# Loads of grouped-query attention: from the wide to the narrow query blocks, with four query buffers

## The chip, the cores and the metric

The kernel runs on one core of a Trainium2 chip. The metric is the device time of one execution in microseconds; the median of the runs shown stands for a kernel. A core has TensorE (matrix products, "PE" in the profile), VectorE ("DVE"), ScalarE ("ACT"), GpSimd ("POOL") and SyncE ("SP"). In this kernel SP does nothing but issue DMAs, one after the other, in the order of the program; all transfers go through this one queue, and 16 DMA engines carry them out.

## What is computed

A gated block on 1024 rows of 512 values: layer norm, then attention with 32 query heads and 8 key/value heads (RMS-normed queries and keys, a linear bias by distance, causal) and a quantized feed-forward network side by side; the attention's output is multiplied by a silu of the network's, and the input is added.

```python
xn = _layernorm(x, axis=-1)
# attention
q = (xn @ Wq.T) ...   # 32 heads of 128
k, v = xn @ Wk.T, xn @ Wv.T ...   # 8 heads of 128: four query heads share one
q, k = _rmsnorm(q, q_norm_w), _rmsnorm(k, k_norm_w)
scores = jnp.einsum('bkgqd,bksd->bkgqs', qg, k) / math.sqrt(HD)
bias = jnp.where(rel > 0, NEG_INF, slopes[:, :, None, None] * rel)
attn = jax.nn.softmax(scores + bias[None], axis=-1)
s = jnp.einsum('bkgqs,bksd->bkgqd', attn, v) ... @ Wo.T
# feed-forward network on xn, weights dequantized by groups of 128
g = _silu((silu(xn @ gate_proj) * (xn @ up_proj)) @ down_proj)
return x + s * g
```

## The kernel before

**Stages.** The feed-forward network runs first (to about 280 us), and its gate silu(...) is stored to the DRAM scratch `gd`. Then come twelve projections (for each pair of key/value heads one "kv" and two "q"), whose results are normed, split into a high and a low 16-bit half, transposed by DMA (`transposed`, L752) and stored to `kd`, `vd` and `qd`. From 423 us on attention runs, at first beside the last two projections.

**Steps of attention.** There are eight groups of heads (g = 0 to 7), each with four blocks of 256 queries (`qb`) and four heads per block and two tiles of 128 queries per head: 256 steps, 32 a group, 8 a block. A step makes the scores of one head and one tile against all keys up to it, so its width is 128 to 1024 keys. Blocks 2 and 3 (widths 640 to 1024) are called wide, blocks 0 and 1 (128 to 512) narrow. Groups 1 to 6 go in the order 2, 3, 0, 1 (`ORDER`): in a group, steps 0 to 15 are wide and 16 to 31 narrow. Group 0 goes 3, 2, 1, 0 and group 7 goes 2, 3, 1, 0. "Step 20 of group 4" below is step 4 * 32 + 20 = 148 of the loop. In the first three groups the bias lets far keys be left out for some heads; groups 3 to 6 have the same full widths.

**One step** (`step(n)`). On TensorE the scores of step n (`scores`), then part of the product with the values for step n - 9 (`values`, `AV_LAG`), then parts of the output projection (`out_proj`). On VectorE `biased` (L1041), one step behind, and `split_lo` (L1074), four steps behind; on ScalarE `exponentials` (L1047) and `split_hi` (L1066). At the end of `split_lo` SP issues the DMA transpose of the split probabilities, L1082, or L1077 for block 0, where one transpose serves both tiles of a head. The product with the values waits for that transpose. So a transpose of step n stands on the queue with the instructions of step n + 4, and its result is wanted at n + 9. The split probabilities lie in five buffers (`P16_BUFS`), the transposed ones in four.

**Other DMAs, all on the same queue.** Per group 512 KB of keys (`load_keys`, L952) at step 4 of the group before, 512 KB of values (`load_values`, L956) at its step 24, and 512 KB of queries a block (`load_queries`, L964), at step 2 of the block before; there are two query buffers. Group 6's queries are stored untransposed, and its loads are two DMA transposes from DRAM a block (L962). Group 7's are never stored: `halves` of the last projection leaves them in SBUF (`last_pairs`), and `last_queries` (L974) transposes them tile by tile into the query buffers, at the steps in `LAST_QUERIES`. When VectorE makes these halves stands in `LAST_PAIRS` (the step is that number plus 8). The output projection's weights of a group are four tiles of 256 KB (`load_wo`, L991), loaded ten steps before the first product, that is at steps 8, 10, 12 and 14 of the group; GpSimd scales them at steps 10 to 16 (L994), ScalarE and GpSimd split them at steps 12 to 18 (L1000, L1001). For the end, `gate_load` (L1131, L1132) brings back 512 KB of the gate and 512 KB of x for each of the four blocks, at steps 211, 219, 235 and 251 (`GATE_LOADS`), into the buffers "f" that the projections used; `gate_partial` on GpSimd uses them at the steps in `GATE_SUMS`.

Of the kernel before, what the change touches and what calls it, by code (L numbers as in the profile page):

```python
# [11 lines left out]
F32 = mybir.dt.float32  # L12
# [10 lines left out]
P = 128  # L23
S = 1024
DM = 512
H = 32
HKV = 8
NH = 4
# [8 lines left out]
NQT = QB // P  # L37
# [10 lines left out]
ORDER = ((2,), (3,), (0,), (1,))  # L48
LAST_ORDER = ((2,), (3,), (1,), (0,))

AV_LAG = 9

KEYS_STEP = 4
VALUES_STEP = 24


LAST_ROOTS = {1: 24, 0: 36}
LAST_PAIRS = {4: 46, 5: 78, 6: 110, 7: 142, 2: 174, 3: 221, 0: 224, 1: 229}
LAST_QUERIES = {4: 217, 5: 219, 6: 225, 7: 227, 2: 233, 3: 235, 0: 241, 1: 243}

WO_SPLIT = 6
WO_SCALE = 8
WO_LOAD = 10

GATE_LOADS = [211, 219, 235, 251]
GATE_SUMS = [227, 235, 251, 259]
PF_BUFS = 5
P16_BUFS = 5
OH_BUFS = 8
# [40 lines left out]
def attention_gated_by_ffn_kernel(ctx, tc, x, gu_w, gu_z, gu_s, dn_w, dn_z, dn_s, wq, wkv, wo, qnw, knw, out):  # L110
    nc = tc.nc
    ve, se, ge, te, sp = nc.vector, nc.scalar, nc.gpsimd, nc.tensor, nc.sync
# [4 lines left out]
    rings = {}  # L117
# [62 lines left out]
    gd = dram.tile([NT, P, DM], F32, name="gd")  # L180
# [645 lines left out]
    for it in range(NI):  # L826
        for tb in range(2):
# [14 lines left out]
            for i in range(4):  # L842
                c = slice(i * P, i * P + P)
# [36 lines left out]
    for tag, cols, bufs in (  # L880
        ("f", 2048, 4),
        ("ss", HT * NH, 3),
        ("ms", HT * NH, 2),
        ("inv", HT * NH, 2),
        ("nwt", HT * NH, 2),
        ("a16", 512, 5),
        ("tr", 512, 5),
        ("k2", 256, 1),
    ):
        ring(tag, fq, cols, bufs)  # L890
# [14 lines left out]
    def pieces(tag, cols):  # L905
        return [slot[:, c : c + cols] for slot in rings[tag].slots for c in range(0, slot.shape[1], cols)]

    wh_pieces = pieces("wh", QB // 2)
    rings["oh"], rings["ol"] = Ring(wh_pieces[:OH_BUFS]), Ring(wh_pieces[OH_BUFS:])
    rings["wor"] = Ring(pieces("wl", DM))  # L910
    free_pieces = pieces("v16", DM // 2) + pieces("sq", DM // 2)
# [2 lines left out]

    def y_rows(t):
        return y_halves[t // HT][:, t % HT * DM : (t % HT + 1) * DM]

    def queue_half(p, half):

# [24 lines left out]
    NB = S // QB  # L944
    blocks = [(g, qbs) for g in range(HKV) for qbs in (FIRST_ORDER if g == 0 else ORDER if g < HKV - 1 else LAST_ORDER)]
    units = [(g, qb, hh) for g, qbs in blocks for hh in range(NH) for qb in qbs]
    kT, vT, qT, woh, wol = {}, {}, {}, {}, {}
    trel, pT, oT, wor = {}, {}, {}, {}

    def load_keys(g):  # L950
        kT[g] = rings["kT"].take(F16, NT, 2, P)
        sp.dma_start(kT[g].rearrange("p t a k -> p t (a k)"), kd[g // 2][:, g % 2])  # L952

    def load_values(g):
        vT[g] = rings["vT"].take(F16, NT, 2, HD)
        sp.dma_start(vT[g].rearrange("p t a d -> p t (a d)"), vd[g])  # L956
# [32 lines left out]
    def load_wo(g, i):  # L989
        wor[g, i] = rings["wor"].take(F32, DM)  # L990
        sp.dma_start(wor[g, i], wo[(g * NH + i) * HD : (g * NH + i + 1) * HD, :])  # L991
# [133 lines left out]

    gates = {}

    def gate_load(qb):
        gx = rings["f"].take(F32, 2, NQT, DM)
        t0 = qb * NQT  # L1130
        sp.dma_start(gx[:, 0], gd[t0 : t0 + NQT].rearrange("t p c -> p t c"))  # L1131
        sp.dma_start(gx[:, 1], x[t0 * P : (t0 + NQT) * P, :].rearrange("(t p) c -> p t c", p=P))  # L1132
        gates[qb] = gx

    def gate_partial(qb, i):

        gx, yt = gates[qb], y_rows(qb * NQT + i)
        ge.tensor_tensor(yt, yt, gx[:, 0, i], ALU.mult)
        ge.tensor_tensor(yt, yt, gx[:, 1, i], ALU.add)
# [17 lines left out]
    nn, BS = len(order), NH * NQT  # L1157
# [2 lines left out]
    begin, free = 0, 0  # L1160
    for k, (g, qbs) in enumerate(blocks[:-1]):
        steps = BS * len(qbs)
        for qb, lead in zip(blocks[k + 1][1], (6, 10) if steps > BS else (2, 5)):
            q_at.setdefault(begin + lead, []).append((blocks[k + 1][0], qb))
        begin += steps
        due = begin + AV_LAG + 1
        n, taken, done = max(free, due), 0, 0
        op_first.setdefault(g, n)
        for qb in qbs:
            for i in range(NQT):  # L1170
                for part in range(NH):
                    op_at.setdefault(n, []).append((g, qb, i, part))
                    if part == NH - 1:
                        acc_at.setdefault(n + 1, []).append((g, qb, i))
                    taken, done = taken + 1, done + 1

                    if taken == 2 or n < due + done:
                        n, taken = n + 1, 0
        free = n + (taken > 0)
    near = [False]  # L1180
    TILES = NT * len(projections)

# [20 lines left out]
    def step(n):  # L1203
        nonlocal last_ps
        if n < nn:
            u, qt = order[n]
            g, qb, hh = units[u]
            for due in q_at.get(n, ()):
                if due[0] < HKV - 1:
                    load_queries(*due)  # L1210
            for t, due in LAST_QUERIES.items():
                if due == n:
                    last_queries(t)
            if g + 1 < HKV:
                if n % (NB * BS) == KEYS_STEP:
                    relative(g + 1)
                    load_keys(g + 1)
                elif n % (NB * BS) == VALUES_STEP:
                    load_values(g + 1)
            scores(u, qt)  # L1220
        done = at(n - AV_LAG - 1)
        done = done[0] if done and done[1] == NQT - 1 else None
        if done is not None:
            heads_hi(done)
        for stage, lag in ((biased, 1), (exponentials, 1), (split_hi, NQT + 1), (split_lo, NQT + 2)):
            advance(stage, n - lag)
        if done is not None:
            heads_lo(done)
        if n < nn + AV_LAG + 1:
            for due in acc_at.get(n, ()):  # L1230
                accumulate(*due)
        finish_step()

        def project():
            for due in op_at.get(n, ()):
                out_proj(*due)

        if at(n - AV_LAG):
            values(*at(n - AV_LAG), project)
        else:  # L1240
            project()
        if done is not None and units[done][:2] == final:
            g, qb, hh = units[done]
            if hh == 0:
                last_ps = [ps2()[:, 0, :] for i in range(NQT)]
            for i in range(NQT):
                out_proj(g, qb, i, hh)
            if hh == NH - 1:
                for due in acc_at.get(nn + AV_LAG + 1, ()):
                    accumulate(*due, other=True)  # L1250
                for i in range(NQT):
                    accumulate(g, qb, i)
        if n in GATE_LOADS:
            gate_load(LAST_ORDER[GATE_LOADS.index(n)][0])
        for i in range(NQT):
            if n - i in GATE_SUMS:
                gate_partial(LAST_ORDER[GATE_SUMS.index(n - i)][0], i)
        for lead, act in ((WO_SPLIT, split_wo), (WO_SCALE, scale_wo), (WO_LOAD, load_wo)):
            for g, first in op_first.items():
                if n + lead - first in range(0, 2 * NH, 2):  # L1260
                    act(g, (n + lead - first) // 2)
# [3 lines left out]
    def project_all(k):  # L1265
        p = projections[k]
        for t in range(NT):
            prepare(k + 1, t)
            if k + 2 < len(projections):
                if t < KT:  # L1270
                    projections[k + 2].load(t)
                n = projections[k + 2].n
                for i in (range(n + 1)[: n // 2], range(n + 1)[n // 2 : n - n // 4], range(n + 1)[n - n // 4 :])[t - 5] if t >= 5 else ():
                    projections[k + 2].squares(i)
            if t == HT:
                p.undo()
                if k == len(projections) - 3:
                    load_keys(0)
                    for qb in blocks[0][1]:
                        load_queries(0, qb)  # L1280
                elif k == len(projections) - 2:
                    load_values(0)
            if (k, t) == (len(projections) - 3, HT + 1):
                wo_squares_sums()

            row = t if k < len(projections) - 1 else (t + HT) % NT
            p.tile(row)
            finish_step()
            if t % HT == HT - 1:
                queue_half(p, row // HT)  # L1290
            c = (k - len(projections) + 2) * NT + t
            if c >= 0:
                for due in q_at.get(c // 2, ()) if c % 2 == 0 else ():
                    load_queries(*due)
                if c == 2 * KEYS_STEP:
                    relative(1)
                    load_keys(1)
                early_tile(c)
# [74 lines left out]
```

## Time and profile before

The three runs took 1016.07, 1020.3 and 1016.7 us, median 1016.7. The profiled execution took 1020.44 us.

| What | us or share |
|---|---|
| Profiled execution / span from first to last instruction | 1020.44 / 1018.6 |
| Granted TensorE clock, mean | 0.989 |
| TensorE / VectorE / ScalarE / GpSimd busy | 95% / 84% / 76% / 42% |
| DMA transposes of probabilities: issued / median to landing | 224 / 3.9 to 4.0 |
| GpSimd's wait for weights of the output projection (L994) | 130.0 |
| Group 4: wide steps / narrow steps | 38.4 / 29.9 |
| Group 6: wide steps / narrow steps | 38.4 / 36.9 |
| From the start of group 7's last block (979.2) to the end | 39.4 |

The profile is a page for one execution: busy times, the span in 40 slices, the chain of work that ended last (followed back from the last instruction to what released each), groups of like instructions, and DMA issues. The trace behind it can be asked for windows, for a timeline and for waits. A window line has start and end, its length, then for each engine the busy time and in brackets the number of instructions, then the granted TensorE clock, the mean busy share of the DMA engines (over 1 where packets of one engine overlap) and GB/s. A timeline line has the start, the time taken (of several merged instructions, from the first's start to the last's end), engine, line and what is written from what. For SP "q" marks its sequencer: the time taken is that of issuing.

### The profile page before, as it was taken

The page shows a single profiled execution, that of the slowest core. Times are in us where ns is not written, and L with a number is a line of the kernel's source. Part 1 is how long each engine was busy: PE and PEld are TensorE (multiplying, and loading weights), DVE is VectorE, ACT ScalarE, POOL GpSimd, SP SyncE. Part 2 cuts the span into 40 slices and gives each one's busy share as a digit, 9 for nine tenths or more (in the row PEclk, how much of TensorE's full clock was granted, in tenths as well). Part 3 has the DMA queues.
Part 4 walks back from the last instruction along what each step waited for, and adds up shares of the span by engine and source line. Part 5 has one row for each costly group of instructions (what it writes and reads, how often), then busy time and mean ns, then how long its engine had stood idle before and what let it go on. Part 6 is the DMA issues. An engine that isn't in the chain of part 4 may idle for free. (4 is left out here: it accounts for less than half of the span.)

```text
span 1018.6 us, 17980 instructions
## 1 busy us (share of the span) xinstructions
PE 964.7 (95%) x5688; PEld 561.8 (55%) x5688; DVE 857.2 (84%) x1764; ACT 775.5 (76%) x2160; POOL 429.4 (42%) x424
## 2 busy tenths in 40 slices
PE   6899999999999999996998999999999999989995
PEld 4344477854444444444555666665676666656562
DVE  7888998728888878877898998987989989969985
ACT  5777745778878887787887987987879978858861
POOL 2588764216666555564235151051241421530722
PEclk9999999999999999999999999999999999999999
DMA  7132359535998999998898999997999999999994
GB/s 251 37 121 93 104 170 310 187 125 163 204 273 190 245 229 215 236 237 202 172 196 161 206 216 183 227 203 158 231 202 191 212 201 190 202 219 198 218 201 108
DMA packets 425063, 195.74 MB, mean 192 GB/s; under 512 B 371522, under 2 KB 382078, under 8 KB 424958
## 3 DMA queue, kind: packets, MB, share of 16 engines
q1 hardware_dynamic: 424958, 194.50, 85.5%
q8 instruction: 46, 0.75, 0.3%
q14 instruction: 59, 0.48, 0.1%
HBM read 76.27 MB, written 27.27 MB: 102 GB/s over the span
## 5 line engine op out<-in xcount | busy, mean ns | idle before, releaser
L1074 DVE SCALAR_TENSOR_TENSOR p<-pf,row,p 128x384 f16<-128x384 f32 (+7 forms) x256 | 208.8, 816 | 20.9 <-ACT p L1066 18.0
L1047 ACT ACTIVATE pf<-pf,row 128x384 f32<-128x384 f32 (+7 forms) x256 | 184.9, 723 | 41.6 <-DVE row L1041 37.3
L1041 DVE CUSTOM_DVE_ANT_0 pf<-s,trel,cs 128x384 f32<-128x384 f32 (+7 forms) x256 | 191.4, 748 | 19.8 <-PE s L153 19.7
L1066 ACT ACTIVATE p<-pf,row 128x384 f16<-128x384 f32 (+7 forms) x256 | 184.0, 719 | 6.3 <-DMA pT<-p 1.4
L151 PE MATMUL s<-kT,qT 128*128 128x512 f16 (+3 forms) x356 | 115.3, 324 | 11.8 <-DVE row L1041 11.5
L994 POOL TENSOR_SCALAR wl<-wl,rvs 128x512 f32<-128x512 f32 x32 | 53.7, 1677 | 149.0 <-DMA wl<-in_wo 130.0
L152 PE MATMUL s<-kT,qT 128*128 128x512 f16 (+3 forms) x356 | 115.4, 324 | 0.0
L153 PE MATMUL s<-kT,qT 128*128 128x512 f16 (+3 forms) x356 | 114.0, 325 | 0.0
L716 POOL TENSOR_TENSOR f<-f,inv 128x512 f32<-128x512 f32 (+1 forms) x96 | 102.1, 1084 | 1.4
L151 PE MATMUL m<-v,wh 128*128 128x512 f16 x248 | 95.0, 383 | 0.0
L153 PE MATMUL m<-v,wh 128*128 128x512 f16 x248 | 94.9, 383 | 0.0
L151 PE MATMUL o<-pT,vT 128*128 128x256 f16 (+1 forms) x302 | 79.6, 264 | 13.9 <-DMA pT<-p 13.7
L151 PEld LDWEIGHTS <-vT 128*128 128x128 f16 x594 | 58.9, 99 | 57.8 <-DMA pT<-p 15.1
L1110 ACT ACTIVATE wh<-o 128x256 f16<-128x256 f32 x128 | 47.7, 373 | 54.4 <-PE o L153 53.8
L152 PEld LDWEIGHTS <-vT 128*128 128x128 f16 x594 | 58.9, 99 | 41.4 <-issue 4.5
L152 PE MATMUL o<-pT,vT 128*128 128x256 f16 (+1 forms) x302 | 79.6, 264 | 0.0
L153 PE MATMUL o<-pT,vT 128*128 128x256 f16 (+1 forms) x302 | 79.3, 264 | 0.0
L151 PE MATMUL o<-wide,vT 128*128 128x256 f16 (+1 forms) x292 | 75.9, 260 | 3.1 <-DMA wide<-p 3.1
L152 PE MATMUL o<-wide,vT 128*128 128x256 f16 (+1 forms) x292 | 75.9, 260 | 0.0
L153 PE MATMUL o<-wide,vT 128*128 128x256 f16 (+1 forms) x292 | 75.7, 260 | 0.0
L151 PE MATMUL m<-wh,xth 128*128 128x512 f16 x192 | 72.8, 379 | 1.2 <-ACT h L869 1.2
L153 PE MATMUL m<-wh,xtl 128*128 128x512 f16 x192 | 72.8, 379 | 0.0
(200 smaller groups left out, 2531.4 us busy)
## 6 DMA issues: line engine op xcount, KB each, us to landing
qd<-tr SPq DMA_DIRECT2D x48, 256.0 KB, 3.3
qT<-qd SPq DMA_DIRECT2D x24, 512.0 KB, 4.4
wide<-in_wq SPq DMA_DIRECT2D x32, 256.0 KB, 3.7
wo_sq<-in_wo SPq DMA_DIRECT2D x8, 1024.0 KB, 7.8
wl<-in_wo SPq DMA_DIRECT2D x32, 256.0 KB, 3.6
gui<-in_gu_w SPq DMA_DIRECT2D x13, 512.0 KB, 3.7
wide<-in_wkv SPq DMA_DIRECT2D x16, 256.0 KB, 3.8
vd<-v SPq DMA_DIRECT2D x8, 512.0 KB, 4.7
```

Of the source, the lines that this page charges most:

```text
L151: te.matmul(ps, lhsT=lh, rhs=rh, start=first, stop=False)
L152: te.matmul(ps, lhsT=lh, rhs=rl, start=False, stop=False)
L153: te.matmul(ps, lhsT=ll, rhs=rh, start=False, stop=last)
L716: ge.tensor_tensor(f, f, ib, ALU.mult)
L994: ge.tensor_scalar(wor[g, i], wor[g, i], rvs[:, g : g + 1], None, ALU.mult)
L1041: ve.tensor_tensor_reduce(p, ps, trel[g][:, S - w :], cs[:, hh : hh + 1], 3e38, ALU.add, ALU.min, least[:, c])
L1047: se.activation(p, p, AF.Exp, bias=least[:, c], scale=-1.0, accum_out=total[:, c])
L1066: se.activation(p16[u, qt][:, :, 0, :], pf[u, qt], AF.Copy, scale=scale[:, qt : qt + 1])
L1074: ve.scalar_tensor_tensor(lo, p, scale, hi, ALU.mult, ALU.subtract)
L1110: se.activation(oh, av_ps[u], AF.Copy, scale=1.0 / P_SCALE)
```

## The change

Four things change.

1. For groups 3 to 7 the loads get new steps, counted in the group before: keys at 20 (was 4), values at 26 (was 24). For groups 3 to 6 the queries of blocks 2, 3, 0, 1 go to steps 21, 22, 28 and 33 (were 26, 34, 42 and 50). The output projection's weights of groups 3 to 6 go to steps 23, 25, 27 and 29 of the group before (were 8, 10, 12 and 14 of their own), those of group 7 to steps 0, 2, 4 and 6 of group 7. Groups 0 to 2 keep their steps.
2. The query ring gets two more buffers, which are the transpose buffers "tr" of the projections under another name.
3. The gate and x loads are cut in four of 256 KB per block: block 2's at steps 20, 22, 24 and 26 of group 3, block 3's at the same steps of group 4, block 1's at those of group 5, block 0's at steps 234 to 240. What uses them keeps its steps.
4. The last projection's late halves move from steps 229, 232 and 237 to 215, 220 and 222, and group 7's transposes of queries from 217 to 243 to 212 to 227.

```diff
-KEYS_STEP = 4
-VALUES_STEP = 24
+RELATIVE_STEP = 4
+LOADS_IN_NARROW = 3
+KEYS_STEP = 4, 20
+VALUES_STEP = 24, 26
+QUERIES_STEPS = (26, 34, 42, 50), (21, 22, 28, 33)
+WO_STEPS = 40, 23, 32
...
-LAST_PAIRS = {4: 46, 5: 78, 6: 110, 7: 142, 2: 174, 3: 221, 0: 224, 1: 229}
-LAST_QUERIES = {4: 217, 5: 219, 6: 225, 7: 227, 2: 233, 3: 235, 0: 241, 1: 243}
+LAST_PAIRS = {4: 46, 5: 78, 6: 110, 7: 142, 2: 174, 3: 207, 0: 212, 1: 214}
+LAST_QUERIES = {4: 212, 5: 213, 6: 216, 7: 217, 2: 220, 3: 221, 0: 226, 1: 227}
...
-WO_LOAD = 10
-
-GATE_LOADS = [211, 219, 235, 251]
-GATE_SUMS = [227, 235, 251, 259]
+GATE_LOADS = {2: [116, 118, 120, 122], 3: [148, 150, 152, 154], 1: [180, 182, 184, 186], 0: [234, 236, 238, 240]}
+GATE_SUMS = {2: 227, 3: 235, 1: 251, 0: 259}
...
-        ("tr", 512, 5),
+        ("tr2", 1024, 2),
+        ("tr1", 512, 1),
...
+    rings["qT"].slots += rings["tr2"].slots
...
+    rings["tr"] = Ring([*pieces("tr2", 512), *pieces("tr1", 512)])
...
-    def gate_load(qb):
-        gx = rings["f"].take(F32, 2, NQT, DM)
-        t0 = qb * NQT
-        sp.dma_start(gx[:, 0], gd[t0 : t0 + NQT].rearrange("t p c -> p t c"))
-        sp.dma_start(gx[:, 1], x[t0 * P : (t0 + NQT) * P, :].rearrange("(t p) c -> p t c", p=P))
-        gates[qb] = gx
+    def gate_load(qb, i):
+        if i == 0:
+            gates[qb] = rings["f"].take(F32, 2, NQT, DM)
+        gx, t = gates[qb], qb * NQT + i // 2
+        sp.dma_start(gx[:, i % 2, i // 2], x[t * P : (t + 1) * P, :] if i % 2 else gd[t])
...
-        for qb, lead in zip(blocks[k + 1][1], (6, 10) if steps > BS else (2, 5)):
-            q_at.setdefault(begin + lead, []).append((blocks[k + 1][0], qb))
+        if g == 0 and blocks[k + 1][0] == 0:
+            q_at.setdefault(begin + 2, []).append((0, blocks[k + 1][1][0]))
...
+    key_at, value_at, wo_at = {}, {}, {}
+    for g in range(HKV):
+        ahead = (g - 1) * NB * BS
+        steps = QUERIES_STEPS[g >= LOADS_IN_NARROW]
+        if g:
+            for step_, (qb,) in zip(steps, ORDER):
+                q_at.setdefault(ahead + step_, []).append((g, qb))
+            key_at[ahead + KEYS_STEP[g >= LOADS_IN_NARROW]] = g
+            value_at[ahead + VALUES_STEP[g >= LOADS_IN_NARROW]] = g
+        for i in range(NH):
+            wo_at[ahead + WO_STEPS[(g >= LOADS_IN_NARROW) + (g == HKV - 1)] + 2 * i] = g, i
```

More of the change, by code (lines that the diff above doesn't have):

```diff
@@ L1214, in step @@
             if g + 1 < HKV:
-                if n % (NB * BS) == KEYS_STEP:
+                if n % (NB * BS) == RELATIVE_STEP:
                     relative(g + 1)
-                    load_keys(g + 1)
-                elif n % (NB * BS) == VALUES_STEP:
-                    load_values(g + 1)
+            if n in key_at:
+                load_keys(key_at[n])
+            if n in value_at:
+                load_values(value_at[n])
             scores(u, qt)
@@ L1252, in step @@
                     accumulate(g, qb, i)
[L1253 to L1258, printed above, removed]
+        for qb, steps in GATE_LOADS.items():
+            if n in steps:
+                gate_load(qb, steps.index(n))
+        for qb, due in GATE_SUMS.items():
+            if 0 <= n - due < NQT:
+                gate_partial(qb, n - due)
+        if n in wo_at:
+            load_wo(*wo_at[n])
+        for lead, act in ((WO_SPLIT, split_wo), (WO_SCALE, scale_wo)):
             for g, first in op_first.items():
@@ L1294, in project_all @@
                     load_queries(*due)
-                if c == 2 * KEYS_STEP:
+                if c == 2 * RELATIVE_STEP:
                     relative(1)
```

## The prediction

> **What bounds the kernel now.** I read the page's busy line first, then windows cut at the wide and narrow steps, then the chain of waits, then SP's timeline.
>
> ```profile
> PE 964.7 (95%) x5688; PEld 561.8 (55%) x5688; DVE 857.2 (84%) x1764; ACT 775.5 (76%) x2160; POOL 429.4 (42%) x424
> GB/s 251 37 121 93 104 170 310 187 125 163 204 273 190 245 229 215 236 237 202 172 196 161 206 216 183 227 203 158 231 202 191 212 201 190 202 219 198 218 201 108
> qT<-qd SPq DMA_DIRECT2D x24, 512.0 KB, 4.4
> wl<-in_wo SPq DMA_DIRECT2D x32, 256.0 KB, 3.6
> ```
>
> TensorE is busy for 95%, so a change of loads can win only what TensorE waits. The windows say where that is; they alternate between a group's wide and narrow steps, from group 3 to group 7.
>
> ```profile
> 631.60:670.00 38.40, 38.40 (x261) 23.74 (x259) 37.47 (x72) 34.69 (x69) 10.33 (x6) 1.00 1.08 209
> 670.00:703.20 33.20, 31.17 (x224) 20.78 (x222) 25.11 (x70) 23.16 (x66) 8.28 (x9) 0.95 0.93 183
> ...
> 741.60:771.50 29.90, 29.60 (x225) 20.19 (x224) 25.31 (x70) 23.28 (x66) 8.32 (x9) 1.00 1.01 197
> ...
> 809.90:840.10 30.20, 29.49 (x225) 20.18 (x223) 25.12 (x68) 23.17 (x66) 8.26 (x9) 1.00 1.03 195
> 840.10:878.50 38.40, 38.40 (x260) 23.74 (x258) 37.49 (x72) 34.69 (x69) 11.15 (x6) 1.00 1.00 196
> 878.50:915.40 36.90, 31.39 (x224) 20.69 (x222) 24.98 (x67) 22.63 (x63) 14.15 (x14) 0.95 1.04 206
> 915.40:958.50 43.10, 40.54 (x261) 24.31 (x259) 42.70 (x78) 34.96 (x70) 15.71 (x9) 0.96 1.08 212
> 958.50:979.20 20.70, 19.58 (x144) 13.22 (x142) 18.14 (x38) 16.83 (x38) 6.41 (x5) 1.00 1.12 197
> ```
>
> Wide steps take 38.40 us in groups 3 and 6 alike, with TensorE never idle and VectorE busy for 37.5: nothing is to be had there. Narrow steps take 29.9 in group 4 with 0.30 idle, so about 29.6 is their floor; group 3 takes 33.2, group 6 takes 36.9. Group 7's wide steps take 4.7 more than 38.40, with VectorE at 42.70 of 43.10. The chain of waits names what TensorE lacked in the narrow steps:
>
> ```profile
> 681.05 5.80 DMA pT<-p
> ...
> 752.40 4.37 DMA pT<-p
> ...
> 884.84 6.06 DMA pT<-p
> ...
> 893.54 5.48 DMA pT<-p
> ```
>
> These are transposes of the last wide steps, wanted at narrow steps 21 to 23. SP's timeline shows why group 6 fares worst, and what stands before the last block's transposes:
>
> ```profile
> 883.19 5.42 SPq L1082 DMA_TRANSPOSE pT<-p  x2
> 888.65 2.98 SPq L962 DMA_TRANSPOSE qT<-qd  x2
> 891.73 4.61 SPq L1082 DMA_TRANSPOSE pT<-p  x2
> ...
> 988.61 0.53 SPq L1131 DMA_DIRECT2D f<-gd  x1
> 989.19 0.48 SPq L1132 DMA_DIRECT2D f<-in_x  x1
> 990.14 1.84 SPq L1077 DMA_TRANSPOSE wide<-p  x1
> ```
>
> VectorE had finished the halves for the transpose at 891.73 by 884.87: it was held 6.9 us behind 2.98 us of query transposes and a slow queue. In group 4 the matching one starts 1.4 us after its halves (749.39 after 748.00), and most others within 0.1 us: there VectorE paces the queue, and an earlier free queue gains about a microsecond, not five.
>
> **The change, part by part: what it removes.** All against the profiled execution's own 1018.6 us of span.
> (a) Narrow steps of groups 3, 4 and 5. Weights (4 x 256 KB) and two query loads (2 x 512 KB) leave the sixteen steps before the late transposes. Those then follow VectorE, and the excess over 29.6 goes: 3.6 + 0.3 + 0.6 = 4.5. Group 2's narrow steps (29.1) wait for VectorE, 0.8 us; nothing is taken.
> (b) Narrow steps of group 6. The query transposes at 888.65 move into group 5, the 1 MB of gate and x at 896.39 into group 3: 36.9 - 29.6 = 7.3.
> (c) Wide steps of group 7. Three halves leave, each a cast of 0.484 us and a subtraction of 0.804 (the rows of L729 and L730 at 512 elements): 3 x 1.29 = 3.9 of VectorE, which is busy there 42.70. That leaves 38.8, just above the 38.40 that TensorE needs; with the bubbles between them I take 39.1, a gain of 4.0 (ends: 0, should another VectorE wait take their place, to 4.7). 1 MB of gate loads and four query transposes leave too; the weights only move eight steps up.
> (d) Group 7's block 1 takes 20.7 with 1.1 idle on transposes; the two query transposes in front of them go: 1.1.
> (e) The end. The transpose at 990.14 stands behind 1 MB and lands after 6.7 us; the two issued at 981.41 and 982.76 land after 3.7 and 3.5. TensorE's idle time for it is 2.3, its landing 3 us late: I take 2.5 (ends 0 and 3.5).
> Sum (a) to (e): 19.4.
> The earlier weights also end GpSimd's wait (130 us in nine waits at L994) and ScalarE's for it (5.7 us at L1000). Both are idle time off the path, taken as nothing; if ScalarE's were on it, it would be 5.7 more. Two more query buffers cost nothing to fill; their memory was the projections' transposes', long read before step 10 first takes it.
>
> **What it adds.** The loads land in the narrow steps behind the last wide transpose: step 19 issues that, and keys stand at step 20. Behind each load are block 0's and block 1's transposes, and for these wait TensorE and, through five probability buffers, ScalarE and then VectorE.
> Bytes first. Group 4's narrow steps move 197 GB/s x 29.9 us = 5.9 MB. Keys, one query load more, four weights and four gate pieces add 0.5 + 0.5 + 1 + 1 = 3 MB or, in bytes, 3.1 MB. That makes 9.0 MB in 29.6 us, 304 GB/s; the page's best slice has 310. So it just fits, with no reserve. Group 2 gets no gates: 2.1 MB more, some 270 GB/s. A single load: 256 KB lands in 3.6 us and 512 KB in 4.4, so 512 KB hold the queue some 1.6 us (estimate: twice the difference).
> The slack: group 4's last transpose of block 0 is issued at 764.95, lands at 768.00 and is used at 771.14, 3.1 us later; the next is issued at 768.14, lands at 771.34 and is used at 774.07, 2.7 later. About 1 MB stands newly before each pair of steps there (weights, a query load, a gate piece), 3.2 us against a slack of 2.7 to 3.1. SP itself has room: 0.55 to 0.67 us an issue, beside transposes of 1.23 each in steps of some 1.5.
> (f) Group 2: 0.3 (ends 0 and 2). (g) Groups 3 and 4: 1.2 each (ends 0, the late loads hidden by the slack, and 5, all of the 9.6 us of added transfer less two slacks). (h) Group 5 loads group 6's queries by DMA transposes, six before its end at 1.3 us of SP each instead of three loads at 0.57: 6.1 us more on SP, of which the gaps between issues take about half: 3 (ends 0 and 7.3, which is what group 6 pays for such a pair today). (i) Group 6: keys, six query transposes of 1.26 us and VectorE's 3.9 us in a stretch where it is busy 25.0 of 29.6, so it reaches 28.9, nearly full: 2 (ends 0 and 7).
> Sum: 0.3 + 2.4 + 3 + 2 = 7.7; the ends are 0 and 26.
> For scale, a rule: the Trainium skill (DMA: Bandwidth & Descriptors, Latency and other measured facts) gives DMA transposes 261 GB/s where the middle dimension is not contiguous, and its section Anatomy of one DMA a variable part of bytes / 436 GB/s. Taking 4.3 MB of group 4's narrow bytes as transposes and the other 4.7 as loads, that makes an estimate of 16.5 + 10.8 = 27.3 us, which would fit with 2 us to spare and put (g) at 0; the row's 310 GB/s has no transposes to speak of in it, and the slower of the two is kept.
> The clock prices a wait a second time. Group 3's narrow steps lose 3.6 us for 2.0 idle, at a granted clock of 0.95; group 4's and 5's, with waits of 0.3 and 0.7, lose no more than these at 1.00. The new waits are nearer to those, so 7.7 stands; at group 3's ratio of 1.8 it would be 13.9. The skill (TensorE: Matmul & The Clock Gate, Part 1: The HAM clock gate) says that the clock halves after an idle window of about 3.4 us. By that rule, too, waits this short are not paid twice.
>
> **The numbers.** 1018.6 - 19.4 + 7.7 = 1006.9 of span. The profiled execution took 1.8 more than its span (1020.44): 1008.7. It lies 3.7 above the median of 1016.7; group 3's stall, which its like in groups 4 and 5 do not have, is about that size, and it is among what goes. So I carry the time over without a shift: **1008.5 us**, 8.2 below the median.
>
> **Rivals.**
> *The room in the narrow steps is used up* (20%). Every load falls due before the queue has caught up, and (f) to (i) come near 16: 1020.4 - 19.4 + 16 = 1017, no change. For it: 304 of 310 GB/s, and a DMA share already at 1.01 to 1.04 in these steps. Against it: the share passes 1.08 in wide steps without TensorE waiting.
> *The loads were hidden anyway* (12%). In groups 3 to 5 VectorE, not the queue, makes the transposes late, (a) is zero, (c) half: 1020.4 - 12.9 + 4 = 1011.5. For it: most transposes start within 0.1 us of their halves. Against: 5.8 us of transfer in group 3 where 3 to 4 is usual.
> *Slower: SP's order in the narrow steps* (13%). One mechanism: transposes of blocks 0 and 1 are pushed past their 2.7 to 3.1 us, the five probability buffers stay full, ScalarE and VectorE stop, and the score matmuls after them, as group 6 shows today at 7.3 us. If groups 3 to 6 each pay that: 1020.4 - 19.4 + 4 x 7.3 + 0.3 = 1030.5. It decides once loads and query transposes ahead of one transpose pass 3 us.
> *The forecast* (55%): its own range is 1002 to 1013, from (f) to (i) near 1 and near 12.
>
> The overall range is 1000 to 1020: below, all gains at no cost (1020.4 - 19.4 = 1001), above, the first rival with some to spare; part of the slower case, a tenth, and a little below are left out. About 0.5% (5 us, 1011.6 and 1021.8) is what a measurement can tell from no change here. Faster by more: most of the forecast's 55%, half of the second rival and a little of the first, 0.60. Same: 0.26. Slower: 0.14, the last rival and the tail of the first.
>
> **What would show it.** Windows: narrow steps of groups 3 and 6 at 30 to 32 us, group 7's wide steps near 39, the stretch from the last block on at some 37. The chain should no longer name transposes at the ends of wide blocks; if it names those of blocks 0 and 1, or ScalarE waiting for pT at L1066, the costs were too low. SP's timeline should show late transposes following the halves within 0.1 to 1.5 us. I am wrong if narrow steps of groups 3 to 5 pass 33 us, or if group 7's wide steps stay at 43.

## The result, and the profile after

The changed kernel takes 1021.21 us, the one before 1017.33 (medians of 20 runs each on the same chips); the ratio is 1.0041, 95% interval 1.0028 to 1.0054. It is slower by 0.4%, where 0.8% faster was forecast. The profiled execution after took 1021.26 us, span 1019.5. From the page, the busy line and the shares of the chain that ended last, by engine:

```profile
PE 962.9 (94%) x5688; PEld 560.1 (55%) x5688; DVE 859.9 (84%) x1764; ACT 775.9 (76%) x2160; POOL 426.0 (42%) x424
...
PE 32%; DMA 6%; DVE 3%; ACT 3%; issue 2%; SPq 2%; POOL 1%; DVEq 0%; ACTq 0%
```

TensorE's share fell by one point. In the chain DMA has 6% (4% before), and SP's queue, which did not appear, has 2%: the wait for transposes did not go, it grew. The windows of the profile after, cut as before (narrow steps of group 2, then wide and narrow steps of groups 3 to 6, then group 7's wide steps, its block 1, and the last block to the end):

```profile
603.26:633.10 29.84, 28.61 (x215) 18.88 (x213) 25.34 (x71) 23.35 (x67) 8.14 (x9) 1.00 1.09 235
633.10:672.26 39.16, 38.58 (x261) 23.66 (x259) 37.28 (x70) 34.72 (x67) 10.29 (x6) 1.00 0.99 190
672.26:701.73 29.47, 29.47 (x224) 20.14 (x222) 25.14 (x70) 23.20 (x66) 8.22 (x9) 1.00 1.07 270
701.73:742.04 40.31, 38.58 (x260) 23.66 (x258) 38.02 (x72) 34.75 (x69) 10.29 (x6) 1.00 0.96 176
742.04:772.28 30.24, 29.79 (x225) 20.18 (x223) 25.80 (x71) 23.58 (x67) 8.22 (x9) 1.00 1.09 251
772.28:812.78 40.50, 38.75 (x260) 23.57 (x258) 37.32 (x70) 34.72 (x67) 10.83 (x6) 1.00 1.04 183
812.78:847.80 35.02, 31.13 (x225) 20.69 (x223) 25.55 (x70) 23.22 (x66) 8.28 (x9) 0.95 1.07 225
847.80:888.82 41.02, 38.75 (x261) 23.57 (x259) 37.75 (x71) 34.66 (x69) 10.29 (x6) 1.00 0.99 175
888.82:919.88 31.06, 29.83 (x225) 20.23 (x222) 28.83 (x73) 22.75 (x64) 15.25 (x15) 1.00 1.10 200
919.88:959.80 39.92, 38.85 (x259) 23.61 (x259) 39.06 (x73) 35.29 (x70) 13.53 (x9) 1.00 1.08 208
959.80:979.03 19.23, 19.23 (x144) 13.28 (x141) 17.41 (x38) 15.73 (x38) 5.49 (x4) 1.00 1.07 193
979.03:1019.50 40.47, 29.38 (x188) 16.74 (x185) 24.69 (x54) 12.59 (x42) 13.75 (x13) 0.89 0.47 109
```

Read against the windows before: narrow steps of group 3 fell from 33.2 to 29.5, of group 6 from 36.9 to 31.1, group 7's wide steps from 43.1 to 39.9, its block 1 from 20.7 to 19.2. But the wide steps of groups 3 to 6, 38.4 in each before, now take 39.2, 40.3, 40.5 and 41.0; group 5's narrow steps rose from 30.2 to 35.0, and the end from 39.4 to 40.5. The DMA rate in the narrow steps of groups 2 to 5 rose to 225 to 270 GB/s, and in the wide steps of groups 3 to 6 it fell to 175 to 190. Cut by blocks (from the timeline, from a block's first score matmul to the next block's):

| Block | group 3 | group 4 | group 5 | group 6 |
|---|---|---|---|---|
| 0, before / after | 19.5 / 16.8 | 17.2 / 16.7 | 17.5 / 16.7 | 23.7 / 16.7 |
| 1, before / after | 13.7 / 12.7 | 12.7 / 13.6 | 12.7 / 18.3 | 13.2 / 14.4 |
| 2 of the next group, before / after | 16.6 / 18.5 | 16.6 / 18.7 | 16.6 / 19.2 | 17.4 / 18.1 |

Block 0 has lost every wait, 11.1 us over the four groups. The two blocks after it pay: block 1 gains 1.0 in group 3 and loses 7.7 in groups 4 to 6, block 2 of the next group loses 7.4 in all, together 14.1. The chain of waits of the profile after names these places:

```profile
699.46 6.72 DMA wide<-p
...
824.11 1.02 SPq L958
...
825.66 1.23 SPq L968
826.94 2.57 SPq L968
...
833.21 1.31 SPq L968
...
835.30 4.83 DMA wide<-p
...
847.94 3.11 DMA wide<-p
...
856.62 4.81 DMA pT<-p
...
931.52 5.13 DMA pT<-p
```

The DMA lines are transposes of blocks 0 and 1, wanted eight or nine steps later; the late transposes of wide steps that the chain named before are gone. In group 5 the chain runs through SP itself: the issue of the keys (L958) and of group 6's query transposes (L968). SP's timeline of the profile after, in group 5's narrow steps, shows the queue:

```profile
819.63 4.43 SPq L1088 DMA_TRANSPOSE pT<-p  x2
824.11 1.02 SPq L958 DMA_DIRECT2D kT<-kd  x1
825.19 0.43 SPq L1138 DMA_DIRECT2D f<-gd  x1
825.66 3.85 SPq L968 DMA_TRANSPOSE qT<-qd  x2
829.68 1.23 SPq L1083 DMA_TRANSPOSE wide<-p  x1
830.95 3.56 SPq L968 DMA_TRANSPOSE qT<-qd  x2
834.56 0.58 SPq L1138 DMA_DIRECT2D f<-in_x  x1
835.30 1.23 SPq L1083 DMA_TRANSPOSE wide<-p  x1
...
843.28 3.21 SPq L968 DMA_TRANSPOSE tr<-qd  x2
846.61 2.56 SPq L1088 DMA_TRANSPOSE wide<-p  x2
```

From 822 to 858 us SP issues without a pause. VectorE had finished the halves for the transposes issued at 829.68, 835.30, 837.80, 841.38 and 846.61 at 824.3, 827.8, 831.2, 836.3 and 838.4: they are 5.3, 7.5, 6.6, 5.1 and 8.2 us late, against the 2.7 to 3.1 us that they can be.

### The profile page after: what moved, and what is told of

Read it like the earlier page. It is cut to its first block, busy times and chain, and to the rows that moved or that the text cites. A ratio compares the mean times of both kernels' runs of the same rounds, so it can differ in the third digit from the quotient of the medians.

```text
span 1019.5 us, 17972 instructions
## 1 busy us (share of the span) xinstructions
PE 962.9 (94%) x5688; PEld 560.1 (55%) x5688; DVE 859.9 (84%) x1764; ACT 775.9 (76%) x2160; POOL 426.0 (42%) x424
## 5 line engine op out<-in xcount | busy, mean ns | idle before, releaser
L1053 ACT ACTIVATE pf<-pf,row 128x384 f32<-128x384 f32 (+7 forms) x256 | 185.0, 723 | 38.6 <-DVE row L1047 35.2
L153 PEld LDWEIGHTS <-vT 128*128 128x128 f16 x594 | 58.4, 98 | 54.2 <-DMA wide<-p 8.7
L153 PE MATMUL o<-pT,vT 128*128 128x256 f16 (+1 forms) x302 | 78.5, 260 | 6.2 <-DMA pT<-p 6.2
L153 PE MATMUL s<-kT,qT 128*128 128x512 f16 (+2 forms) x228 | 76.6, 336 | 6.1 <-DVE row L1047 5.9
L154 PE MATMUL o<-pT,vT 128*128 128x256 f16 (+1 forms) x302 | 78.3, 260 | 0.0
L155 PE MATMUL o<-pT,vT 128*128 128x256 f16 (+1 forms) x302 | 78.1, 260 | 0.0
L154 PE MATMUL s<-kT,qT 128*128 128x512 f16 (+2 forms) x228 | 76.7, 336 | 0.0
L1000 POOL TENSOR_SCALAR wl<-wl,rvs 128x512 f32<-128x512 f32 x32 | 52.5, 1641 | 57.5 <-DMA wl<-in_wo 57.5
L155 PE MATMUL s<-kT,qT 128*128 128x512 f16 (+2 forms) x228 | 75.1, 336 | 0.0
```

Of the source, the lines that this page charges most:

```text
L153: te.matmul(ps, lhsT=lh, rhs=rh, start=first, stop=False)
L154: te.matmul(ps, lhsT=lh, rhs=rl, start=False, stop=False)
L155: te.matmul(ps, lhsT=ll, rhs=rh, start=False, stop=last)
L1000: ge.tensor_scalar(wor[g, i], wor[g, i], rvs[:, g : g + 1], None, ALU.mult)
L1053: se.activation(p, p, AF.Exp, bias=least[:, c], scale=-1.0, accum_out=total[:, c])
```

## The experiments

Two theories. *Queue*: the loads' issues stand ahead of the probabilities' transposes on SP, group 6's query transposes worst. *Bytes*: the 16 DMA engines are full in the narrow steps, and what is added there lands late whatever its order. Times are compared with runs of the kernel before on the same chip; the first profile of the change is "after". The changed kernel has no runs on those chips and stands beside them with its ratio of 1.0041.

**Group 6's queries back.**

```diff
-        steps = QUERIES_STEPS[g >= LOADS_IN_NARROW]
+        steps = QUERIES_STEPS[LOADS_IN_NARROW <= g < HKV - 2]
```

> The changed kernel with group 6's query loads (two DMA transposes a block) back at steps 26, 34, 42 and 50, all else as changed. Queue theory (the loads' issues stand ahead of the probabilities' transposes on SP; group 6's query transposes, 1.2 to 2.6 us of SP each, are the worst): the narrow steps of group 5 plus the first wide block of group 6, 35.0 + 19.2 us after the change, fall to some 30 + 17.5, and group 6's narrow block 0 rises from 16.7 to 18 to 20, not to the 23.7 of before, since the weights and gates stay away from it; about 3 to 6 us faster than the changed kernel, near 1016. Byte theory (the DMA engines are full, order does not matter): the same bytes move, group 5's narrow steps stay above 33, time within 2 us of the changed kernel.

Measured: ratio 0.9995 (0.9971 to 1.0018). Windows of this run: group 5's narrow steps, then blocks 2 and 3 of group 6, then its narrow steps:

```profile
817.63:848.77 31.14, 29.52 (x224) 20.21 (x222) 26.18 (x72) 23.60 (x67) 8.93 (x10) 1.00 1.11 226
848.77:865.38 16.61, 16.61 (x119) 10.44 (x117) 15.77 (x33) 14.78 (x33) 3.67 (x2) 1.00 1.08 195
865.38:887.18 21.80, 21.80 (x144) 13.30 (x142) 21.17 (x36) 19.44 (x35) 5.69 (x4) 1.00 1.13 194
887.18:920.88 33.70, 30.16 (x225) 20.09 (x222) 27.46 (x73) 22.54 (x64) 15.12 (x15) 1.00 1.10 196
```

The first two fall from 54.2 to 47.8, the last rises from 31.1 to 33.7 (block 0 takes 18.5): some 4 us net, as the queue theory has it. Where group 6's queries are loaded makes the difference between 0.4% slower and no change. Block 2 of group 4, which this edit does not reach, took 20.5 here and 18.5 after (its granted clock was 0.92 here, with TensorE busy for 18.47 us instead of 16.79). So one block in one execution is good to about 2 us, and sums over several say more.

**The same loads without the transpose.** The two DMA transposes of a block of group 6 are replaced by one plain load, at the same steps.

```diff
-        if g == HKV - 2:
-            for i in range(NQT):
-                sp.dma_start_transpose(...)
-            return
```

> The changed kernel, with group 6's queries loaded by one plain DMA of 512 KB a block instead of two DMA transposes, at the same steps; they stay untransposed, so group 6's attention is computed from wrong queries. Same bytes, 0.6 us of SP instead of 2.6 to 4. Queue theory: group 5's narrow steps and group 6's block 2 together fall from 54.3 to what groups 4 and 5 take at the same place, 30.2 + 18.7 = 49. Byte theory: 53 to 55, unchanged.

Measured in one execution: group 5's narrow steps and block 2 of group 6 take 31.07 + 18.33 = 49.4, with the same bytes, as the queue theory said. The queue's timeline at the place shown above, of this run:

```profile
826.19 1.05 SPq L958 DMA_DIRECT2D kT<-kd  x1
827.29 0.43 SPq L1134 DMA_DIRECT2D f<-gd  x1
827.76 0.43 SPq L966 DMA_DIRECT2D qT<-qd  x1
828.36 1.33 SPq L1079 DMA_TRANSPOSE wide<-p  x1
829.74 0.77 SPq L966 DMA_DIRECT2D qT<-qd  x1
```

A query load holds SP 0.43 to 0.77 us instead of 3.6 to 3.9, and the first transpose follows the keys after 2.2 us instead of 5.6. So 4.8 of the 54.2 us come from loading the queries by transposes, and not from the number of bytes (1.8 of them are a slow clock in the profile after, see below). The transposed form also cuts the bytes into other packets; the test does not separate SP's issue time from the engines' work on these.

**Fewer bytes, as many issues.** The gate and x pieces of groups 3 to 5 cut to an eighth of their columns.

```diff
-        sp.dma_start(gx[:, i % 2, i // 2], x[...] if i % 2 else gd[t])
+        c = slice(0, DM if qb == 0 else DM // 8)
+        sp.dma_start(gx[:, i % 2, i // 2, c], x[..., c] if i % 2 else gd[t][:, c])
```

> The changed kernel with the gate and x pieces of groups 3 to 5 cut to an eighth of their columns: as many issues on SP, an eighth of the bytes; three of the four query blocks are gated with wrong values. Byte theory: block 2 of groups 4 and 5, 18.5 and 18.7 after the change, falls to 16.6 to 17.4. Queue theory (the issues count): 18 or more in both. Group 5's narrow steps: 33 to 34 by either, as the query transposes stay.

Measured in one execution: block 2 of groups 4 and 5 at 17.8 and 17.5, 35.3 together. In the three profiles that have the whole gates there (after, and the two above) the sum is 37.0 to 38.7; in the four below that have none there (old steps, wide steps, and the last two) it is 33.7 to 35.2. So this lies between the theories: bytes seem to count in groups 4 and 5, where no query transposes are, but by no more than like executions differ, and how much of the rest is issue time stays open. Group 5's narrow steps and block 2 of group 6 take 53.6 against 54.2.

**The gates back at their old steps.**

```diff
-GATE_LOADS = {2: [116, 118, 120, 122], 3: [148, 150, 152, 154], 1: [180, 182, 184, 186], 0: [234, 236, 238, 240]}
+GATE_LOADS = {2: [211] * 4, 3: [219] * 4, 1: [235] * 4, 0: [251] * 4}
```

> The changed kernel with the gate and x loads back at steps 211, 219, 235 and 251 (as four pieces of 256 KB each, issued together). Byte theory: groups 3 to 5 lose 1 MB each in their narrow steps, so block 2 of groups 4 and 5 falls from 18.5 and 18.7 to about 17 (group 3, which follows narrow steps without gates, takes 17.4 after the change), and group 5's narrow steps from 35.0 to about 33. Queue theory: four issues of 0.45 to 0.6 us less per group, 2 us, gives nearly the same in groups 3 and 4, but group 5 keeps 2/3 of its loss, 33 or more. Either way group 6's narrow steps and the last block get slower again by some 2 to 4 us; total 1018 to 1022.

Measured: ratio 1.0035 (1.0016 to 1.0054), as slow as the change. The profiled execution, at 1019.82 us, was the fastest of the ten; their median is 1023.95. In it block 2 of groups 4 and 5 is at 16.6 and 17.3, group 5's narrow steps at 31.2 (both theories had said 33), but block 2 of group 6 takes 20.9 at a granted clock of 0.92 (sum 52.1 against 54.2), and group 6's narrow steps 33.5 and group 7's wide ones 42.2 give the gain back. The gates cost in the old place as in the new one. Group 7's block 3 stays at 21.8 and block 1 at 19.2 with its gates returned, so these owe their gain to the early halves and queries, not to the gates' leaving.

**The loads on another queue.** Weights and gates are issued by GpSimd.

```diff
-        sp.dma_start(gx[:, i % 2, i // 2], ...)
+        ge.dma_start(gx[:, i % 2, i // 2], ...)
...
-        sp.dma_start(wor[g, i], ...)
+        ge.dma_start(wor[g, i], ...)
```

> The changed kernel with the weights' and the gates' loads issued by GpSimd instead of SP, at the same steps. Same bytes, eight issues fewer on SP per narrow stretch. Queue theory: block 2 of groups 4 and 5 back to 16.6 to 17 and the probabilities' transposes within 1 us of their halves; group 5's narrow steps still above 32, since the query transposes stay on SP; 3 to 5 us faster, near 1017. Byte theory: the lateness stays, block 2 of group 4 at 18 or more, time unchanged within 2 us.

Measured: ratio 1.0146 (1.0119 to 1.0173), slower by far than both theories had said. Block 2 of groups 4 and 5 went to 16.6 in both, as the queue theory said, but block 1 of groups 3 to 6 takes 15.7, 19.6, 23.0 and 21.4, and the granted clock in the narrow steps of groups 4 to 6 is 0.87 to 0.91. SP's timeline of this run, group 5's narrow steps:

```profile
831.42 0.95 SPq L958 DMA_DIRECT2D kT<-kd  x1
832.42 8.04 SPq L968 DMA_TRANSPOSE qT<-qd  x2
840.63 5.03 SPq L1083 DMA_TRANSPOSE wide<-p  x1
845.70 2.66 SPq L968 DMA_TRANSPOSE qT<-qd  x2
```

With fewer issues on SP, SP got slower: two query transposes hold it 8.0 us instead of 3.9, one probability transpose 5.0 instead of 1.2. From 600 to 960 us a weight's 256 KB land after 7.4 us (median; 3.4 from SP). So SP's "issue time" is not fixed by what it issues. The likely reading is that traffic from a second queue takes the DMA engines from the transposes, that SP's time contains waiting for the engines behind it, and that the two theories are two sides of one backlog; the runs show the longer times, not this cause.

**The fourth part alone.** The kernel before with the early halves, early query transposes of group 7 and four query buffers; the diff is that of the change for these names.

> The kernel before with the fourth part of the change alone: four query buffers, the late halves and group 7's query transposes early; keys, values, weights, gates and queries of groups 3 to 6 as before. If group 7's gain is due to these halves (VectorE's 3.9 us): its wide steps fall from 43.1 to about 39.5, block 1 from 20.7 to 19.5 to 20.5; groups 3 to 5 as before; group 6's narrow steps at 36 to 40, with the query transposes of both groups in them. Total 2 to 4 us faster than before if group 6 does not get worse, near 1014; if it does, 1017. Rival (the weights and gates, by their bytes, were what slowed group 7): its wide steps stay above 41.5.

Measured: ratio 1.0027 (1.0 to 1.0054). Block 3 of group 7 falls from 25.7 to 21.8 and block 1 from 20.7 to 19.2, as said, and VectorE is busy for 39.05 us in the wide steps instead of 42.70. But block 2 rises from 17.4 to 21.3 and block 1 of group 6 from 13.2 to 15.7, so the wide steps as a whole stay at 43.1, where 39.5 was expected and the rival had said above 41.5; group 6's block 0 is at 24.3. In block 1 of group 6 the transposes of probabilities start 2.6 to 6.4 us after their halves. The gain of (c) is real and is returned in the stretch that the query transposes moved to, as long as that is full.

**The kernel before once more**, for a second profile.

> The kernel before, unchanged, for a second profile. If the 3.6 us that group 3's narrow steps lost in the first profile are chance, they take 30 to 31 here and the execution about 3 us less; group 6's narrow steps stay at 36 to 37.5 and group 7's wide steps at 43, since these follow from the queue's order and from VectorE's load. If group 3's 33.2 come back, the loss is the kernel's own.

Measured: 1023.73 us, with a median of 1021.75 for seven runs on that chip. Group 3's narrow steps take 30.95, so 2.3 of the 33.2 us of the first profile were chance; group 6's take 38.0 and group 7's wide steps 43.1. The execution is not 3 us shorter, as was expected, but 3.3 longer. From the first score matmul to the last matmul of all, attention takes 588.0 and 588.1 us in the two profiles, so nearly all of the 3.3 lies ahead of it: it begins at 422.9 and 426.1 us.

**The gates into wide steps.** Only this is changed in the changed kernel:

```diff
-GATE_LOADS = {2: [116, 118, 120, 122], 3: [148, 150, 152, 154], 1: [180, 182, 184, 186], 0: ...
+GATE_LOADS = {2: [98, 100, 102, 104], 3: [130, 132, 134, 136], 1: [162, 164, 166, 168], 0: ...
```

> The changed kernel with one move: the gate and x pieces of groups 3 to 5 at wide steps 2, 4, 6 and 8 of the same groups, as in f1_spread. If the narrow steps have no room and the wide ones have some now, block 2 of groups 4 and 5 is at 16.6 to 17.3, block 0 of groups 3 to 5 stays at 16.7, group 5's narrow steps at 32 to 33 (the query transposes stay), block 2 of group 6 at 17 to 20; ratio to before 0.996 to 1.000, some 5 us better than the changed kernel's 1.0041. If group 6's query transposes alone were the cost, the ratio stays above 1.002.

Measured: ratio 0.9979 (0.9956 to 1.0001), 0.6% better than the change for moving 3 MB by 18 steps. Block 2 of groups 4 and 5 takes 16.6 and 17.1, block 0 of groups 3 to 5 stays at 16.7 and block 3 at 21.8; group 5's narrow steps and block 2 of group 6 still take 31.1 + 21.3 = 52.4, the latter above the 17 to 20 expected.

**All three taken together.** The gates as above, group 6's queries spread over block 2 and 3, group 7's query transposes partly earlier:

```diff
+        steps = (26, 34, 37, 40) if g == HKV - 2 else QUERIES_STEPS[g >= LOADS_IN_NARROW]
...
-LAST_QUERIES = {4: 212, 5: 213, 6: 216, 7: 217, 2: 220, 3: 221, 0: 226, 1: 227}
+LAST_QUERIES = {4: 201, 5: 203, 6: 212, 7: 213, 2: 217, 3: 220, 0: 226, 1: 227}
```

> The changed kernel with three moves: the gate and x pieces of groups 3 to 5 at wide steps 2, 4, 6 and 8 of the same groups; group 6's queries at steps 26, 34, 37 and 40; group 7's query transposes for block 2 at steps 201 and 203, for block 3 at 212 and 213, for block 1 at 217 and 220. If queue and bytes in the narrow steps are what gave the gain back, block 2 of groups 4 and 5 returns to 16.6 to 17.4, group 5's narrow steps to about 31, block 2 of group 6 to 17, block 0 of group 6 stays at 16.7 to 17.5, block 2 of group 7 falls below 18; wide block 3 stays at 21.8. Total 5 to 9 us under before, ratio 0.991 to 0.995. If wide steps cannot take the gates (the reason to move loads in the first place), block 0 of groups 3 to 5 is back at 17.2 to 19 and the ratio is 1.0.

Measured: 1012.09 us, ratio 0.9908 (0.9874 to 0.9942), faster than both kernels. Its windows: block 2 of group 4, narrow steps of group 5, blocks 2 and 3 of group 6, its narrow steps, group 7's wide steps:

```profile
701.95:718.57 16.62, 16.62 (x120) 10.44 (x118) 16.33 (x37) 15.05 (x35) 4.61 (x2) 1.00 1.09 236
...
809.00:839.10 30.10, 29.52 (x225) 20.20 (x223) 25.89 (x71) 23.61 (x67) 8.28 (x9) 1.00 1.03 199
839.10:855.71 16.61, 16.61 (x120) 10.44 (x118) 16.32 (x35) 14.95 (x33) 4.41 (x2) 1.00 1.03 191
855.71:879.05 23.34, 22.14 (x144) 13.13 (x142) 21.40 (x36) 19.40 (x35) 5.42 (x4) 1.00 1.14 193
879.05:913.24 34.19, 30.29 (x224) 19.98 (x222) 29.23 (x71) 22.72 (x64) 14.80 (x15) 1.00 1.12 204
913.24:951.92 38.68, 38.66 (x258) 23.75 (x258) 38.25 (x70) 34.83 (x70) 13.04 (x9) 1.00 1.03 200
```

Block 3 of group 6 now pays 1.5 us and its narrow steps take 34.2 where they took 31.1 after the change: SP issues six query transposes from step 198 to 205 (four of group 6's, two of group 7's), and these are too many. One more run takes group 7's two out of there and sets group 6's queries to 26, 34, 37 and 41. Its expectation speaks of eight, of which four leave; the timelines show six and two.

> As e9_gates_wide, and group 6's queries at steps 26, 34, 37 and 41, group 7's query transposes where the change has them. In f1_spread wide block 3 of group 6 (23.3) and block 0 (19.5) paid 4.4 us for eight added transposes: with four of them gone they should take 21.8 to 22.5 and 17 to 18.5, while block 1 and block 2 of group 7 return to some 14.4 and 18. About even with f1_spread or 1 to 2 us better: ratio 0.989 to 0.993. If the ratio is above 0.994, group 7's query transposes in the narrow steps cost more than in the wide ones.

Measured: 1013.24 us, ratio 0.9932 (0.9914 to 0.9951). Block 3 takes 22.4 and block 0 17.7, as expected, and the narrow steps 32.5; group 7's wide steps are back at 40.4. The two runs are even within their intervals. Block 2 of group 4 takes 17.8 with no gates near, where the three runs before it had 16.6 in the same place. By the ratios either beats the change by 1% and more.

## Why the prediction was wrong

**What was right.** The gains (a) to (d): 16.9 us forecast, 17.5 measured (block 0 of groups 3 to 6 11.1, block 1 of group 3 1.0, block 3 of group 7 3.9, its block 1 1.5). Each floor was met: 16.7, 21.8 and 19.2 us. Some 2.3 of the 17.5 are luck: group 3's blocks 0 and 1 took 18.3 and 12.7 us in the second profile of the kernel before, not 19.5 and 13.7.

**(e), the end.** 2.5 us of gain forecast, 1.0 of loss in the profile. The transpose there did land sooner, after 3.0 us instead of 6.7, but the chain of the profile after runs through VectorE and ScalarE in that stretch and names no DMA. The chain of the kernel before names none there either, between 985 and 1001 us; that path was not looked for. TensorE then idled into a slow clock: a window of the kernel before with the matmuls behind that idle time, then three of the profile after:

```profile
1000.97:1009.03 8.06, 8.06 (x47) 4.23 (x48) 2.20 (x4) 0.77 (x3) 0.00 (x0) 1.00 0.26 66
```

```profile
990.00:1000.20 10.20, 7.59 (x51) 4.21 (x50) 9.28 (x23) 4.87 (x17) 4.55 (x4) 1.00 0.48 103
1000.20:1003.67 3.47, 3.47 (x11) 1.49 (x12) 0.00 (x0) 0.00 (x0) 0.00 (x0) 0.51 0.64 151
1003.67:1009.90 6.23, 6.23 (x38) 3.27 (x36) 2.20 (x4) 0.77 (x3) 0.00 (x0) 1.00 0.11 42
```

For 3.47 us the granted clock is 0.51, which costs about half of that; before, the same matmuls ran at 1.00 throughout. It is not in every execution: from the start of the last block to the end of the last matmul it took 32.8 us after, but 31.1 to 31.6 in six other runs with the change's end, and 31.8 and 32.0 in the two profiles of the kernel before. So the loss is chance, and the gain without it 0.2 to 0.9 us. The Trainium skill (TensorE: Matmul & The Clock Gate, Part 1: The HAM clock gate) gives a window of about 3.4 us and half the clock; both are seen here, though the idle time before it was broken into pieces of at most 1.0 us, not one of 3.4 us.

**(f) to (i), the price, is the step that failed.** 7.7 us were forecast, 16.7 measured: (f) 1.6 for 0.3, (g) 4.9 for 2.4, (h) 8.3 for 3, (i) 1.9 for 2. The rows were at hand: 3.1 MB, 304 of 310 GB/s, 6.1 us more of SP in group 5. The error is in what was done with them. Each load was set against the slack of the one transpose behind it, 2.7 to 3.1 us, and "of which the gaps between issues take about half" was assumed for (h). But the queue does not empty between steps 19 and 35: SP issues without a pause from 684 to 714 us in group 3, from 751 to 786 in group 4 and from 822 to 858 in group 5. So each transpose carries the delay of the loads before it: 5.3 to 8.2 us from step 17 to step 24 of group 5. In group 4, where those from step 19 on had started within 0.5 us of their halves, the transposes of steps 17 to 31 now start 1.6 to 4.2 us late. A backlog is a sum over the stretch, not a sequence of slacks. That the query transposes are its worst part in group 5 is shown by putting them back (54.2 to 47.8 us) and by loading them plainly (to 49.4), that the gates are a part by moving them (1.0041 to 0.9979). "Waits this short are not paid twice" did not hold there either: in block 1 of group 5, with a wait of 2.9 us, the granted clock is 0.91 and TensorE is busy for 14.46 us where 12.69 were enough before. That is 1.8 us of (h); in the other windows of groups 2 to 7 up to the last block the clock stays at 1.00.

**The fit of the bytes.** "It just fits, with no reserve" set a mean over the stretch against 310 GB/s from a stretch without DMA transposes. The two blocks of a narrow stretch differ: windows of the profile after, blocks 0 and 1 of group 3,

```profile
672.26:689.05 16.79, 16.79 (x143) 12.71 (x141) 14.56 (x39) 13.48 (x38) 8.22 (x9) 1.00 1.04 207
689.05:701.73 12.68, 12.68 (x83) 7.42 (x81) 10.57 (x31) 9.71 (x29) 0.00 (x0) 1.00 1.12 353
```

In groups 3 to 5 block 0 moves 193 to 207 GB/s, no more than the 203 to 208 of before; the added bytes go through in block 1, at 353, 323 and 246 GB/s where it was 149 to 183. So 310 is no ceiling, but over a whole narrow stretch no run passed 272, and of the 9.0 MB counted 7.6 to 8.0 were through at its end, after 29.5 to 35.0 us. The estimate of 27.3 us by the two rates of the Trainium skill (DMA: Bandwidth & Descriptors) was thus further off than the row; the second of them, bytes / 436 GB/s, stands in a section on transfers that GpSimd issues, and these were issued by SP.

**The time carried over without a shift.** The two profiled executions of the kernel before lie 3.1 and 2.0 us above the medians of their chips' runs, that of the change within 0.1. The profiles thus show a loss of 0.8 us of span, the medians 3.9. All of the 0.8 lies ahead of group 2, before any load has moved; from there to the end the change takes 444.9 us, and the kernel before 444.9 and 443.6 in its two profiles. Group 3's stall was counted as a gain against a median that mostly lacks it. Where the rest of the 3 us lies, in an execution of before that is as fast as its median, no profile shows; it stays open.

**The rival that came.** "The room in the narrow steps is used up", with costs near 16, at 20%. It said 1017, and with (e) lost it would have said 1020.5. The chances leaned on gains that were well founded, but the costs had ends of 0 and 26 and were taken near the lower one. The third rival had the mechanism of group 5, transposes of blocks 0 and 1 pushed past their slack, which cost 8.3 us there where it had said 7.3; it set that price on four groups, and one paid it. The prediction's own sign of being wrong, narrow steps over 33 us, came in group 5 (35.0).

## What to carry to other kernels

When loads move out of a stretch where a queue is late, add up what the stretch that receives them must issue and move in all, against its whole length, and carry the delay forward from one transfer to the next; slack of single transfers is good only for queues that empty in between. Cheap places are those whose load has just become lighter: here the wide steps, from which the other moves had taken loads, took the 3 MB of gates, and blocks 3 and 0 of groups 3 to 5 stayed at 21.8 and 16.7 us. A DMA transpose counts for several plain loads on the queue (3.6 to 3.9 us of SP for two, 0.43 to 0.77 for the plain load of the same bytes).

## What the runs showed of the hardware

- Issuing weights and gates from GpSimd's queue beside SP's slowed the kernel by 1.5%: the median landing of a weight's 256 KB in attention went from 3.4 to 7.4 us, and SP's transposes took up to 5.0 us to issue instead of 1.2. The Trainium skill (DMA: Bandwidth & Descriptors, Issuing engines are not separate DMA queues) says that this saves only the sequencer's issue time; here it cost more than it saved.
- In the profile after, a DMA transpose of 256 KB from DRAM held SP 1.2 to 2.6 us, a plain load of 512 KB of queries mostly 0.4 to 0.6, at most 1.8.
- With the early weights GpSimd's wait for them went from 130.0 to 57.5 us. What that alone is worth no run shows.
- Over 12.68 us (block 1 of group 3 after) the DMA engines moved 353 GB/s, transposes of probabilities among it, with TensorE never idle.
